# Position network of an attention layer: VectorE's and ScalarE's instructions in a written order, additions two pairs ahead, weighted sums a pair later, first-layer scalings one at a time

## The chip, the cores and the metric

The kernel runs on one core of a Trainium2 chip. A core has five engines that run beside each other and wait for one another by semaphores: TensorE (PE in the profile, its weight loads PEld), VectorE (DVE), ScalarE (ACT), GpSimd (POOL) and SyncE (SP, which issues transfers). The time is that of one execution on the device in microseconds; the median of several runs is compared. Before the change it is 3746.29 us (three runs, 3746.23 to 3746.82).

## The reference

Four layers run one behind the other; the change lies in the first, a deformable attention on x of 2 images, 512 channels, 32 by 32. In it, each of 16 heads (2 images by 8 groups) has 1024 queries and 64 keys. To every score a bias is added which a small network computes from the position of query and key:

```python
pos = grid_q[:, :, None, :] - grid_kv[:, None, :, :]
bias = jnp.sign(pos) * jnp.log1p(jnp.abs(pos))
bias = jax.nn.relu(bias @ cpb_w1 + cpb_b1)      # 2 -> 128
bias = jax.nn.relu(bias @ cpb_w2 + cpb_b2)      # 128 -> 128
bias = (bias @ cpb_w3 + cpb_b3)                 # 128 -> 1
sim = jnp.einsum('bhid,bhjd->bhij', qh, kh) + bias
attn = jax.nn.softmax(sim, axis=-1)
```

That is 16 x 64 x 1024 positions through a hidden layer of 128 by 128, all in float32. The output projection, an MLP and the other three layers (a deformable convolution, a linear attention and an ordinary attention) follow and are not touched.

## The kernel before

The part that matters is `biased_scores` (L828), called the position network here. It works on NP = 8 pairs of heads ("head pairs", index p), and in each on 32 rows j in steps of two. A step (p, j) holds four pairs of keys (t = 0 to 3): the heads 2p and 2p+1, and the keys j, j+1 and j+32, j+33. Counted through, that is 128 steps and 512 pairs; pair n = 64p + 2j + t.

For one key, `hidden` (L862) makes the first layer's output, a tile of 128 hidden units by 1024 queries. The position is separable in x and y, so the first layer is a sum of an x part and a y part: an addition on VectorE (L869), with both parts broadcast, then a relu, on VectorE for the keys 3, 8 and 13 of each sixteen (L876), else on ScalarE (L878). Six such tiles `h` exist, so three pairs.

For a pair, `second_layer` (L881) does the 128 by 128 product on TensorE (L889) in two halves of the output units, `ph`, each of two PSUM banks; three such tiles rotate. A matmul has a tile of 32 columns of the array, and four of them run side by side, two for each key. ScalarE reads the first half with bias and relu into `lo` (L899, two tiles) and the second into `hi` (L901, six tiles, scaled by the size of the last layer's weight). VectorE adds them, `hi = lo * low_w + hi` (L902), which halves the last layer's depth. `last_layer` (L904) then multiplies the four `hi` of a step into `sim` on TensorE (L910). It is called for a step only behind the second pair of the next step.

The x and y parts come from `first_layer` (L511): for a group (p, q) of sixteen rows j it loads four tiles `ab` of 128 by 1024 from DRAM (L521, on SP's queue), and then multiplies each by a weight and adds a bias, in place, on ScalarE (L534). Two groups fit into the pool `cpb_ab`. The next group is called for at j % 16 == 8.

At j = 0 the `sim` of the head pair before is stored (L932, VectorE), at j = 16 the scores themselves are added in (L922, TensorE). In the last four head pairs the softmax of the first four is done beside the network, one step of it after every fourth step (`next(beside)`). `Softmax.parts` (L994): eight transposes on TensorE into a `ph` tile and the maximum (L1012) and the subtraction (L1014) on VectorE; the exponential on ScalarE (L1016); the sum, reciprocal and product on VectorE (L1018 to L1021); at last eight transposes back and a copy on ScalarE (`turn`, L1033).

The order of instructions is set in two ways. A scheduler orders the instructions of an engine by its own view of when their inputs are ready, unless a block `manual_schedule` names that engine: then they stand as the program writes them. Before the change this block names TensorE alone, for the whole of this part. Each engine runs its queue in order, so an instruction that waits holds up all behind it.

Of the kernel before, what the change touches and what calls it, by code (L numbers as in the profile page):

```python
# [11 lines left out]
F32 = mybir.dt.float32  # L12
AF = mybir.ActivationFunctionType
# [497 lines left out]
def first_layer(net, pool, feat, p, q):  # L511

    nc, parts = net.nc, {}
    for i in (2 * p, 2 * p + 1):
        parts[i, q] = []
        for a in range(2):
            t = pool.tile([128, 32, 32], F32, name="ab", tag=f"ab{a}")
            row = feat[16 * a + i : 16 * a + i + 1, :]  # L520
            nc.sync.dma_start(  # L521
                out=t.rearrange("p (u j) i -> p u (j i)", u=2),
                in_=bass.AP(
                    tensor=row.tensor,
                    offset=row.offset + 512 * q,
                    ap=[[0, 128], [HW, 2], [1, 512]],
                ),
            )
            parts[i, q].append(t)
    yield parts  # L530
    for i in (2 * p, 2 * p + 1):
        for a, t in enumerate(parts[i, q]):
            bias = net.vec("cpb_b1") if a == 0 else 0.0
            nc.scalar.activation(t, t, AF.Identity, bias=bias, scale=net.vec("cpb_w1", a))  # L534
    yield parts


class DepthwiseConv:
# [80 lines left out]
def queries_keys_values(net, bn, simT, q_flat, q_pad, kbd, val, feat, first):  # L619
# [5 lines left out]
    with ExitStack() as ctx:  # L625
# [59 lines left out]
        with ExitStack() as part:  # L685
# [109 lines left out]
                            skip_group_check=True,  # L795
                        )
            with net.tc.issue_after(last.ins):
                done = next(weigh)
            for h in range(2):
                r = 64 * h  # L800
                (nc.vector.tensor_copy, nc.scalar.copy)[h](
# [5 lines left out]
            for w, out, factor in ((kw, kbd, 64**-0.5), (vw, val, 1.0)):  # L807
                for q in range(2):
# [14 lines left out]
                        ALU.mult,  # L823
                    )
    return done


def biased_scores(net, q_pad, kbd, feat, w2, simT, first, parts, load_weights):  # L828
# [12 lines left out]
    with ExitStack() as ctx:  # L841
# [20 lines left out]
        nc.vector.tensor_copy(w3[0:64, 30:31], sign[0:64, :])  # L862
        nc.vector.tensor_copy(w3[64:128, 31:32], sign[64:128, :])

        def hidden(i, j, on_vector):
            at_x, at_y = parts[i, j % 32 // 16]
            k = 16 * (j // 32) + j % 16
            h1 = hid1.tile([128, HW], F32, name="h1", tag="h1")
            nc.vector.tensor_tensor(  # L869
                h1.rearrange("p (y x) -> p y x", x=32),  # L870
                at_x[:, k : k + 1, :].to_broadcast([128, 32, 32]),
                at_y[:, k, :].unsqueeze(2).to_broadcast([128, 32, 32]),
                ALU.add,
            )
            if on_vector:
                nc.vector.tensor_scalar(h1, h1, 0.0, None, ALU.max)  # L876
            else:
                nc.scalar.activation(h1, h1, AF.Relu)  # L878
            return h1

        def second_layer(pair):  # L881

            phs = []
            for k in range(2):
                ph = ps_h.tile([128, HW], F32, name="ph", tag="ph")
                for n in range(2):
                    for t in range(4):
                        c0 = 64 * k + 32 * (t % 2)
                        nc.tensor.matmul(  # L889
                            ph[32 * t : 32 * t + 32, half(n)],  # L890
                            lhsT=w2[:, c0 : c0 + 32],
                            rhs=pair[t // 2][:, half(n)],
                            start=True,
                            stop=True,
                            skip_group_check=True,
                        )
                phs.append(ph)
            lo = lows.tile([128, HW], F32, name="lo", tag="lo")
            nc.scalar.activation(lo, phs[0], AF.Relu, bias=b2_lo)  # L899
            hi = highs.tile([128, HW], F32, name="hi", tag="hi")  # L900
            nc.scalar.activation(hi, phs[1], AF.Relu, bias=size_b, scale=size)  # L901
            nc.vector.scalar_tensor_tensor(hi, lo, low_w, hi, ALU.mult, ALU.add)  # L902
            return hi

        def last_layer(sim, j, sums):


            for n in range(2):
                for t in range(4):
                    nc.tensor.matmul(  # L910
                        sim[32 * t : 32 * t + 32, half(n)],
                        lhsT=w3[:, 30 - j : 62 - j],
                        rhs=sums[t][:, half(n)],
                        start=(j == 0),
                        stop=(j == 30),
                        skip_group_check=True,
                    )
# [13 lines left out]
        def store(p, sim):  # L931
            nc.vector.tensor_scalar(simT[:, p, :], sim, net.vec("cpb_b3"), None, ALU.add)  # L932
# [11 lines left out]
        soft = Softmax(net, simT, one, two_banks)  # L944
        beside = chain(*(soft.steps(p) for p in range(CC)))

        pending = None
        sim = None
        hidden_done = 0
        for p, j in [(p, j) for p in range(NP) for j in range(0, 32, 2)]:  # L950
            if j % 16 == 8:
                nxt = 2 * p + j // 16 + 1
                if nxt < 2 * NP:
                    parts.update(list(first_layer(net, first, feat, *divmod(nxt, 2)))[-1])
            sums = []
            for t in range(4):
                pair = []
                for k in range(2):
                    key = j + 32 * (t % 2) + k
                    pair.append(hidden(2 * p + t // 2, key, hidden_done % 16 in (3, 8, 13)))  # L960
                    hidden_done += 1
                sums.append(second_layer(pair))
                if t == 1 and pending is not None:
                    last_layer(sim, *pending[1:])
            if j == 0:
                if pending is not None:
                    store(pending[0], sim)
                sim = ps_sim.tile([128, HW], F32, name="sim", tag="sim")
            elif j == 16:
                scores(p, sim)  # L970
                if p == NP - 1:
                    weights = load_weights()
            pending = (p, j, sums)
            if p >= CC and j % 8 == 4:
                next(beside, None)
        for _ in beside:
            pass
        last_layer(sim, *pending[1:])
# [4 lines left out]
class Softmax:  # L983
# [18 lines left out]
    def parts(self, p):  # L1002
        nc, one = self.net.nc, self.one
        pt = self.banks("pt").rearrange("p (h j) -> p h j", j=64)
        for c in range(8):
            nc.tensor.transpose(
                pt[:, 2 * c : 2 * c + 2, :].rearrange("p h j -> p (h j)"),
                self.simT[:, p, 128 * c : 128 * c + 128],
                self.net.cst("ident"),
            )  # L1010
        m = one("m", 16)
        nc.vector.tensor_reduce(m, pt, AX.X, ALU.max)  # L1012
        e = one("e", HW).rearrange("p (h j) -> p h j", j=64)
        nc.vector.tensor_tensor(e, pt, m.unsqueeze(2).to_broadcast([128, 16, 64]), ALU.subtract)  # L1014
        yield e
        nc.scalar.activation(e, e, AF.Exp)  # L1016
        s = one("s", 16)
        nc.vector.tensor_reduce(s, e, AX.X, ALU.add)  # L1018
        yield e
        nc.vector.reciprocal(s, s)  # L1020
        nc.vector.tensor_tensor(e, e, s.unsqueeze(2).to_broadcast([128, 16, 64]), ALU.mult)  # L1021
        yield e
# [1182 lines left out]
```

## Time and profile before

| | |
|---|---|
| median of the runs | 3746.29 us |
| the profiled execution's own time | 3739.29 us |
| its span, first to last instruction | 3737.4 us |
| mean granted TensorE clock | 0.991 |
| TensorE busy | 3634.7 us (97%) |
| VectorE busy | 2763.5 us (74%) |
| ScalarE busy | 2605.5 us (70%) |
| first and last start of the second layer (L889) | 86.8 and 2116.7 us |
| scalings of `ab` (L534) | 64, of 1.13 to 1.29 us, from 74.3 us on |

The profile lists groups of equal instructions: line, engine, operation, output and inputs, shape, count, busy time and mean duration, then the idle time of the engine just before them and what ended most of it. A timeline row gives start, duration, engine, line, operation, count, and in brackets the idle time before it with its releaser. In the slices of the span (forty, each 93.4 us) TensorE is at nine tenths or more from the second slice to the 32nd, VectorE and ScalarE from the second to the 22nd, which is the position network. A row of windows has start and end, length, then busy time and count of PE, PEld, DVE, ACT and POOL, the granted clock, the share of the DMA engines and GB/s. Matmuls are pipelined and their ends are modelled: a busy share of TensorE is not its rate.

### The profile page before, as it was taken

What the parts mean: (1) busy time and instruction counts of PE and PEld (TensorE: products, weight loads), DVE (VectorE), ACT (ScalarE), POOL (GpSimd) and SP (SyncE); (2) the same over time, 40 slices, a digit from 0 to 9 for tenths busy, and PEclk for the clock granted to TensorE, in tenths of its full rate; (3) what the DMA queues carried; (4) which work ended last, traced back from release to release, by engine and by line L of the source; (5) the groups of instructions that cost most, each with busy time, mean ns of one, the idle gap of its engine ahead of it and who ended that gap; (6) DMA issues with size and microseconds to landing.
All of it is one profiled execution on the core that took longest, in us unless ns stands there. A gap on an engine that the chain in (4) does not pass through costs nothing. (4 is left out here: it accounts for less than half of the span.)

```text
span 3737.4 us, 59880 instructions
## 1 busy us (share of the span) xinstructions
PE 3634.7 (97%) x24332; PEld 1381.4 (37%) x24332; DVE 2763.5 (74%) x3178; ACT 2605.5 (70%) x2877; POOL 436.0 (12%) x692
## 2 busy tenths in 40 slices
PE   7999999999999999999999999999997999989999
PEld 4432322232223232322323344444443455534434
DVE  6999999999999999999999611321257457277776
ACT  7999999999999999999999621021113223257875
POOL 0000000000000000000000000000126024036655
PEclk9999999999999999999999999999998999999999
DMA  3000000000000000000001100012345547036665
GB/s 114 1 24 24 24 1 23 24 24 1 24 24 13 12 24 24 1 24 24 24 1 58 51 12 0 9 33 85 101 137 197 175 144 252 34 102 176 172 180 173
DMA packets 95718, 237.87 MB, mean 64 GB/s; under 512 B 21220, under 2 KB 26852, under 8 KB 92244
## 3 DMA queue, kind: packets, MB, share of 16 engines
q0 software_dynamic: 38160, 112.73, 9.8%
q1 hardware_dynamic: 56132, 117.36, 9.5%
q8 instruction: 193, 3.16, 0.4%
q10 hardware_dynamic: 1152, 3.96, 0.3%
q14 instruction: 81, 0.66, 0.1%
HBM read 157.16 MB, written 9.70 MB: 45 GB/s over the span
## 5 line engine op out<-in xcount | busy, mean ns | idle before, releaser
L889 PE MATMUL ph<-h,w_t 128*32 128x512 f32 x16384 | 1808.1, 593 | 15.7 <-ACT lo L899 6.5
L869 DVE TENSOR_TENSOR h<-ab 128x1024 f32<-128x1024 f32 x1024 | 1205.3, 1217 | 67.5 <-PE ph L889 66.5
L889 PEld LDWEIGHTS ph<-h,w_t 128*32 128x32 f32 x16384 | 547.5, 110 | 1240.0 <-issue 1014.6
L878 ACT ACTIVATE h<-h 128x1024 f32<-128x1024 f32 x832 | 872.2, 1067 | 46.1 <-DVE h L869 42.7
L902 DVE SCALAR_TENSOR_TENSOR hi<-lo,low_w,hi 128x1024 f32<-128x1024 f32 x512 | 654.1, 1278 | 31.7 <-ACT hi L901 30.3
L901 ACT ACTIVATE hi<-ph,size_b,size 128x1024 f32<-128x1024 f32 x512 | 621.3, 1214 | 16.7 <-PE ph L889 12.5
L899 ACT ACTIVATE lo<-ph,vec_t 128x1024 f32<-128x1024 f32 x512 | 571.9, 1117 | 5.9 <-PE ph L889 5.5
L1568 PE MATMUL po<-fold,turned 128*128 128x512 f32 x576 | 270.0, 613 | 3.1 <-DVE dfacc L1576 2.9
L1136 ACT ACTIVATE h<-ph,vec_t 128x512 f32<-128x512 f32 x64 | 44.0, 687 | 312.1 <-PE ph L1128 311.6
L910 PE MATMUL sim<-hi,w 128*32 128x512 f32 x2048 | 251.0, 592 | 0.0
L1197 POOL MEMSET pad<- 128x2312 f32 x2 | 4.1, 2032 | 2075.3 <-PE ph L889 2075.3
L1491 POOL DMA_INDIRECT got<-table,idx x144 | 169.7, 1178 | 555.7 <-DVE sum L1515 273.7
L1128 PE MATMUL ph<-xn,room 128*128 128x512 f32 x512 | 231.0, 594 | 0.0
L1117 PE MATMUL acc<-h,mlp_w_t 128*128 128x512 f32 x512 | 229.8, 592 | 0.0
L1515 DVE SCALAR_TENSOR_TENSOR sum<-got,wts,sum 128x256 f32<-128x256 f32 x432 | 184.6, 479 | 44.8 <-ACT sum L1511 42.1
L2115 DVE TENSOR_REDUCE m<-pl 128x1 f32<-128x1024 f32 x128 | 150.6, 1218 | 84.5 <-PE pl L2003 84.4
L2049 POOL DMA_DIRECT2D aT<-e x344 | 169.0, 499 | 207.0 <-DVE s L2132 97.2
L2121 ACT ACTIVATE e<-pl,m 128x1024 f32<-128x1024 f32 x86 | 95.7, 1114 | 82.8 <-DVE m L2115 56.6
L1568 PEld LDWEIGHTS po<-fold,turned 128*128 128x128 f32 x576 | 108.0, 198 | 114.9 <-issue 109.9
L1542 ACT COPY turned<-pt 128x512 f32<-128x512 f32 x72 | 42.0, 583 | 150.7 <-PE pt L1536 150.7
L1117 PEld LDWEIGHTS acc<-h,mlp_w_t 128*128 128x128 f32 x512 | 97.3, 190 | 122.5 <-issue 122.0
L1128 PEld LDWEIGHTS ph<-xn,room 128*128 128x128 f32 x512 | 96.6, 191 | 117.8 <-issue 117.2
(265 smaller groups left out, 2885.7 us busy)
## 6 DMA issues: line engine op xcount, KB each, us to landing
ab<-feat_d SPq DMA_DIRECT2D x64, 512.0 KB, 4.2
aT<-e SPq DMA_DIRECT2D x344, 64.0 KB, 2.6
aT<-e POOLq DMA_DIRECT2D x344, 64.0 KB, 2.5
room<-in_dc_w_dram SPq DMA_DIRECT2D x9, 1024.0 KB, 4.8
aT<-x_all SPq DMA_DIRECT2D x96, 64.0 KB, 2.7
aT<-x_all POOLq DMA_DIRECT2D x96, 64.0 KB, 2.4
dc_w_t<-in_dc_w_dram SPq DMA_DIRECT2D x5, 1024.0 KB, 4.9
room<-in_mlp_w_dram SPq DMA_DIRECT2D x1, 4096.0 KB, 15.5
```

The source lines that it names most:

```text
L869: nc.vector.tensor_tensor(h1.rearrange("p (y x) -> p y x", x=32), at_x[:, k : k + 1, :].to_broadcast([128, 32, 32]), at_y[:, k, :].unsquee ...
L878: nc.scalar.activation(h1, h1, AF.Relu)
L889: nc.tensor.matmul(ph[32 * t : 32 * t + 32, half(n)], lhsT=w2[:, c0 : c0 + 32], rhs=pair[t // 2][:, half(n)], start=True, stop=True, skip_ ...
L899: nc.scalar.activation(lo, phs[0], AF.Relu, bias=b2_lo)
L901: nc.scalar.activation(hi, phs[1], AF.Relu, bias=size_b, scale=size)
L902: nc.vector.scalar_tensor_tensor(hi, lo, low_w, hi, ALU.mult, ALU.add)
L910: nc.tensor.matmul(sim[32 * t : 32 * t + 32, half(n)], lhsT=w3[:, 30 - j : 62 - j], rhs=sums[t][:, half(n)], start=(j == 0), stop=(j == 30 ...
L1117: nc.tensor.matmul(accs[oc], lhsT=self.w2[:, m, 128 * oc : 128 * oc + 128], rhs=hs[m], start=(m == 0), stop=(m == 15),)
L1128: nc.tensor.matmul(ph, lhsT=self.w1[:, k, 128 * m : 128 * m + 128], rhs=xn[:, k, :], start=(k == 0), stop=(k == CC - 1),)
L1491: nc.gpsimd.indirect_dma_start(out=g.rearrange("p s i -> p (s i)"), out_offset=None, in_=f.table.rearrange("(r t) s i -> r t (s i)", t=2), ...
L1515: nc.vector.scalar_tensor_tensor(t[:, q, :], g[:, s, :], w, t[:, q, :], ALU.mult, ALU.add)
L1568: nc.tensor.matmul(self.out, lhsT=turned[:, at : at + 128], rhs=self.folded.w[k][:, i, :], start=(k == 0 and i == 0), stop=(k == 8 and i = ...
```

## The change

The loop of `biased_scores` now stands in a `manual_schedule` block for VectorE and ScalarE, so their order is that of the program. In the order:

- The two additions of a pair and its relus on VectorE (`added`) come two pairs ahead of the second layer that uses them. The relus on ScalarE stand one behind `lo` and one behind `hi` of the pair two before (`rectified`).
- The weighted sum of a pair comes behind the additions in the next pair (`behind`), no longer with its own.
- The next group's `ab` tiles are called for at j % 16 == 2, and scaled one at a time at the start of the steps j % 16 = 6, 8, 10 and 12 (`next_parts`, and the `yield` that moves into the loop of `first_layer`). The second group's scalings, which before stood ahead of the network, now run inside it.
- In the softmax, the sum of the exponentials moves from the step of the exponential to the next one.

The choice of keys whose relu is on VectorE, the buffers, and the order on TensorE, GpSimd and SyncE stay; each engine has the same instructions as before.

```diff
 def first_layer(...):
         for a, t in enumerate(parts[i, q]):
             bias = net.vec("cpb_b1") if a == 0 else 0.0
             nc.scalar.activation(t, t, AF.Identity, bias=bias, scale=net.vec("cpb_w1", a))
-    yield parts
+            yield parts
...
             with net.tc.issue_after(last.ins):
-                done = next(weigh)
+                done = list(weigh)[-1]
...
+        def added(n):
+            i, first_key = pairs[n]
+            made = []
+            for j in (first_key, first_key + 1):
...
+                nc.vector.tensor_tensor(
+                    h1.rearrange("p (y x) -> p y x", x=32),
...
+                made.append(h1)
+            for u, h1 in enumerate(made):
+                if (2 * n + u) % 16 in ON_VECTOR:
+                    nc.vector.tensor_scalar(h1, h1, 0.0, None, ALU.max)
+            return made
+
+        def rectified(n, u):
+            if n in hiddens and (2 * n + u) % 16 not in ON_VECTOR:
+                h1 = hiddens[n][u]
+                nc.scalar.activation(h1, h1, AF.Relu)
...
+        def weighted(lo, hi):
             nc.vector.scalar_tensor_tensor(hi, lo, low_w, hi, ALU.mult, ALU.add)
...
+        def next_parts(nxt):
+            making = first_layer(net, first, feat, *divmod(nxt, 2))
+            parts.update(next(making))
+            yield
+            yield from making
+
+        pending, sim, hiddens, behind, making = None, None, {}, None, iter(())
+        ahead = 2
+        with net.tc.manual_schedule(
+            engines={mybir.EngineType.DVE, mybir.EngineType.Activation}
+        ):
+            for n in range(ahead):
+                hiddens[n] = added(n)
+                for u in range(2):
+                    rectified(n, u)
+            for p, j in [(p, j) for p in range(NP) for j in range(0, 32, 2)]:
+                if j % 16 == 2:
+                    nxt = 2 * p + j // 16 + 1
+                    if nxt < 2 * NP:
+                        making = next_parts(nxt)
+                if j % 16 > 4 or j % 16 == 2:
+                    next(making, None)
+                sums = []
+                for t in range(4):
+                    n = 64 * p + 2 * j + t
+                    phs = second_layer(hiddens.pop(n))
+                    if n + ahead < len(pairs):
+                        hiddens[n + ahead] = added(n + ahead)
+                    lo = lows.tile([128, HW], F32, name="lo", tag="lo")
+                    nc.scalar.activation(lo, phs[0], AF.Relu, bias=b2_lo)
+                    rectified(n + ahead, 0)
+                    hi = highs.tile([128, HW], F32, name="hi", tag="hi")
+                    nc.scalar.activation(hi, phs[1], AF.Relu, bias=size_b, scale=size)
+                    rectified(n + ahead, 1)
+                    if behind is not None:
+                        weighted(*behind)
+                    behind = lo, hi
+                    sums.append(hi)
+                    if t == 1 and pending is not None:
+                        last_layer(sim, *pending[1:])
...
+            weighted(*behind)
...
         nc.scalar.activation(e, e, AF.Exp)
+        yield e
         s = one("s", 16)
         nc.vector.tensor_reduce(s, e, AX.X, ALU.add)
-        yield e
         nc.vector.reciprocal(s, s)
```

More of the change, by code (lines that the diff above doesn't have):

```diff
@@ L825, in queries_keys_values @@
     return done
+ON_VECTOR = 3, 8, 13
 def biased_scores(net, q_pad, kbd, feat, w2, simT, first, parts, load_weights):
@@ L863, in biased_scores @@
         nc.vector.tensor_copy(w3[64:128, 31:32], sign[64:128, :])
[L865 to L877, printed above, removed]
+        pairs = [
+            (2 * p + t // 2, j + 32 * (t % 2))
+            for p in range(NP)
+            for j in range(0, 32, 2)
+            for t in range(4)
+        ]
+        def added(n):
+            i, first_key = pairs[n]
+            made = []
+            for j in (first_key, first_key + 1):
+                at_x, at_y = parts[i, j % 32 // 16]
+                k = 16 * (j // 32) + j % 16
+                h1 = hid1.tile([128, HW], F32, name="h1", tag="h1")
+                nc.vector.tensor_tensor(
+                    h1.rearrange("p (y x) -> p y x", x=32),
+                    at_x[:, k : k + 1, :].to_broadcast([128, 32, 32]),
+                    at_y[:, k, :].unsqueeze(2).to_broadcast([128, 32, 32]),
+                    ALU.add,
+                )
+                made.append(h1)
[6 more added lines that the diff above has]
+                h1 = hiddens[n][u]
                 nc.scalar.activation(h1, h1, AF.Relu)
-            return h1
         def second_layer(pair):
@@ L897, in second_layer @@
                 phs.append(ph)
[L898 to L901, printed above, removed]
+            return phs
+        def weighted(lo, hi):
             nc.vector.scalar_tensor_tensor(hi, lo, low_w, hi, ALU.mult, ALU.add)
-            return hi
         def last_layer(sim, j, sums):
@@ L945, in biased_scores @@
         beside = chain(*(soft.steps(p) for p in range(CC)))
[L947 to L975, printed above, removed]
@@ new lines, in next_parts @@
+        def next_parts(nxt):
[37 more added lines that the diff above has]
+                        last_layer(sim, *pending[1:])
+                if j == 0:
+                    if pending is not None:
+                        store(pending[0], sim)
+                    sim = ps_sim.tile([128, HW], F32, name="sim", tag="sim")
+                elif j == 16:
+                    scores(p, sim)
+                    if p == NP - 1:
+                        weights = load_weights()
+                pending = (p, j, sums)
+                if p >= CC and j % 8 == 4:
+                    next(beside, None)
+            weighted(*behind)
```

## The prediction

> **What bounds the kernel now.** I read the page first (busy times, slices, groups), then the windows, then TensorE's and ScalarE's timelines inside the position network, where the whole change lies.
>
> ```profile
> span 3737.4 us, 59880 instructions
> PE 3634.7 (97%) x24332; PEld 1381.4 (37%) x24332; DVE 2763.5 (74%) x3178; ACT 2605.5 (70%) x2877; POOL 436.0 (12%) x692
> L889 PE MATMUL ph<-h,w_t 128*32 128x512 f32 x16384 | 1808.1, 593 | 15.7 <-ACT lo L899 6.5
> L869 DVE TENSOR_TENSOR h<-ab 128x1024 f32<-128x1024 f32 x1024 | 1205.3, 1217 | 67.5 <-PE ph L889 66.5
> L878 ACT ACTIVATE h<-h 128x1024 f32<-128x1024 f32 x832 | 872.2, 1067 | 46.1 <-DVE h L869 42.7
> L902 DVE SCALAR_TENSOR_TENSOR hi<-lo,low_w,hi 128x1024 f32<-128x1024 f32 x512 | 654.1, 1278 | 31.7 <-ACT hi L901 30.3
> L901 ACT ACTIVATE hi<-ph,size_b,size 128x1024 f32<-128x1024 f32 x512 | 621.3, 1214 | 16.7 <-PE ph L889 12.5
> L899 ACT ACTIVATE lo<-ph,vec_t 128x1024 f32<-128x1024 f32 x512 | 571.9, 1117 | 5.9 <-PE ph L889 5.5
> ```
>
> The network runs from 84 to 2121 us. The window over it:
>
> ```profile
> 84.00:2121.00 2037.00, 2021.40 (x18562) 627.04 (x18563) 1936.54 (x1764) 1965.79 (x1922) 2.02 (x1) 1.00 0.06 19
> ```
>
> PE is busy 2021.4 us of 2037, DVE 1936.5 and ACT 1965.8: three engines within 5%, so the order in which they serve each other matters. TensorE's timeline tells which one sets the pace:
>
> ```profile
> 330.35 1.90 PE L910 MATMUL sim<-hi,w 128*32 128x512 f32 x16
> 332.07 10.69 PE L889 MATMUL ph<-h,w_t 128*32 128x512 f32 x96
> 343.05 3.64 PE L889 MATMUL ph<-h,w_t 128*32 128x512 f32 x32 [0.30 <-ACT hi L901]
> 346.51 1.90 PE L910 MATMUL sim<-hi,w 128*32 128x512 f32 x16
> 348.23 5.33 PE L889 MATMUL ph<-h,w_t 128*32 128x512 f32 x48
> 354.02 8.96 PE L889 MATMUL ph<-h,w_t 128*32 128x512 f32 x80 [0.46 <-ACT lo L899]
> 362.80 1.90 PE L910 MATMUL sim<-hi,w 128*32 128x512 f32 x16
> ```
>
> One L910 row opens each step of four key pairs. Undisturbed steps are 15.45 us apart (378.25, 393.70, 409.15 follow), most of the 127: 36 groups of four matmuls at 0.429 us, TensorE's own rate. A pair is thus 3.43 us, the last layer 1.72. The two steps shown are 16.16 and 16.29: 0.71 and 0.84 lost. Added over the timeline, beyond 15.45 and beyond the scores (2.02 a head pair) and softmax transposes (1.16 a set), the losses are 25.8 us: 11.7 in the first four head pairs and 14.0 in the last four. Of the 25.8, 20.1 lie at the 14 places where four scalings of `ab` run (some 1.4 each), 5.6 behind the softmax steps. That 25.8 is all that any order can win here. ScalarE at such a place:
>
> ```profile
> 338.70 1.07 ACT L878 ACTIVATE h<-h 128x1024 f32<-128x1024 f32 x1
> 339.64 1.13 ACT L899 ACTIVATE lo<-ph,vec_t 128x1024 f32<-128x1024 f32 x1
> 340.64 1.27 ACT L534 ACTIVATE ab<-ab,vec_t 128x1024 f32<-128x1024 f32 x1
> 341.77 1.23 ACT L901 ACTIVATE hi<-ph,size_b,size 128x1024 f32<-128x1024 f32 x1
> 342.86 1.15 ACT L899 ACTIVATE lo<-ph,vec_t 128x1024 f32<-128x1024 f32 x1
> ```
>
> Starts give the time that each holds the engine: relu 0.95, `lo` 1.00, `hi` 1.09, scaling 1.04 to 1.13 (I take 1.09). The `hi` that ends at 343.00 releases TensorE at 343.05, so ScalarE to TensorE takes 0.05. The other way is read where ScalarE waits:
>
> ```profile
> 2112.18 1.11 ACT L899 ACTIVATE lo<-ph,vec_t 128x1024 f32<-128x1024 f32 x1 [1.54 <-PE ph L889]
> 2113.90 1.21 ACT L901 ACTIVATE hi<-ph,size_b,size 128x1024 f32<-128x1024 f32 x1 [0.60 <-PE ph L889]
> ```
>
> That pair's matmuls start at 2110.21 (call it S): `lo` can start at S+1.97, `hi` at S+3.69. An addition waiting for the freed `h` starts 0.24 behind (2105.28 against 2105.04).
>
> **The change, part by part.** No instruction is added or removed, and the order on TensorE, POOL and SP stays; only DVE and ACT are reordered, in the network alone. So the `ab` loads keep their place in SP's queue; they land 4.2 us after issue, and each scaling is two steps (31 us) or more behind: no price.
>
> *Steady order.* ScalarE now runs, for pair n: `lo`(n), relu(n+2,0), `hi`(n), relu(n+2,1): 1.00+0.95+1.09+0.95 = 3.99 us against TensorE's 3.43. VectorE takes 3 of 16 relus, so in the pairs 2, 4 and 7 of each eight ScalarE has 3.04. TensorE's last layer (1.72) follows pairs 1 and 5. Let the lag be how late `lo`(n) starts behind S+1.97. A full pair adds 0.56, a short one takes 0.39, a last layer takes 1.72. From zero at pair 2: 0.33 at pair 3 (its `hi` before waited for TensorE), 0.88 at 4, 0.49 at 5, 0 at 6, 0.56 at 7, 0.16 at 0, 0.72 at 1, then zero. Two limits: `lo`(n) must be read before the second half of pair n+1 takes its PSUM buffer (three rotate), lag+1.97+1.11+0.05 < 5.15, so lag < 2.02; and relu(n+2,1), done at S+6.12+lag, must precede pair n+2 at S+6.87, so lag < 0.75 where no last layer lies between. The second is tight once in eight pairs, at pair 3: 0.33 against 0.75. DVE needs two additions 2.27, weighted sum 1.20 and at times a relu 0.61: 3.47 or 4.08 a pair against 3.43, its lag stays under 1.4 and clears at each last layer; a sum a pair later is still 2.3 us ahead of its last layer. Steady state costs nothing, as before; cover 0.42 us at pair 3, 64 times.
>
> *Scalings one to a step.* They stand ahead of pair 4, 0, 4, 0. Lags: 0.88+1.09 = 1.97 at pair 4, just inside 2.02; then 1.58, 0.42 (pair 6), 0.98, and with the second scaling 1.68, 2.24 (a last layer follows, so free), 1.06, 0.67 (limit 0.75), and with the third 0.67+0.56+1.09 = 2.32: 0.30 too late. The fourth stays inside. So 0.30 a group where some 1.4 stood; 15 groups (the second group's, until now ahead of the network, comes into it): 4.5 us. Ends: 0, and 1.55 (0.71+0.84 above). I take 0.30, reached with this trace's own durations.
>
> *Softmax steps,* one after every fourth step of the last four head pairs. First: maximum and subtraction (2.4 us) stand in DVE's queue and wait for the transposes; two additions, a relu and the sum of pair 3 are behind, and it comes some 0.1 us before the last layer needs it: 0.05 each. Second: the exponential lands on a lag of 1.28 left by the fourth scaling: 1.28+0.95-2.02 = 0.21, three times, and 1.6 the first time, with the table load. Third: sum, reciprocal and product (2.69 us by their starts) push the sum of pair 3 to 11.2 us behind that pair's start, the last layer wants it at 10.3: 0.9, four times. Fourth: the copy fits in the transposes' own 1.16. Storing a head pair (1.28 on DVE) leaves 0.6 of cover. Together 0.2+2.2+3.6 = 6.0, ends 0 and 12.
>
> The table load is a row of 1.28 us at 1149.34, and the exponential starts at 1150.63, right behind. [...]
>
> *Start and end.* ScalarE loses four scalings ahead of the first pair, but that pair waits for DVE's first addition at 84.40, behind the copies of `val`: 0, ends plus and minus 1. The end is the same chain of `hi`, sum, last layer.
>
> Sum: 4.5+6.0 = 10.5 us of losses for 25.8: 15.3 less. The profiled execution took 3739.3 us (span 3737.4 and 1.9 around it), so 3724.0; the median shown is 7.0 above it: 3731.0.
>
> **The rivals.** *Nothing of the 25.8 stays* (chance 0.12): the lags run 0.3 lower, every wait is covered: 3720.5. For it: 0.30 is a small overshoot. Against: the 0.9 behind the third softmax step.
>
> *Scalings cost the same one by one as together* (0.16): ScalarE owes 4.4 us a group whatever the spacing, and the four steps have 15.6 us of its work in 15.45; 15 times 1.43 and 6.0 are 27.5, 1.7 over: 3748. Against: the pairs' own lag returns to zero in between, up to 0.88 only.
>
> *Slower: ScalarE's fixed order misses pair 5* (0.14). At pair 3 relu(5,1) stands behind `hi`(3), which waits for TensorE; a scheduler may move it, a fixed order may not. Cover 0.42; each 0.1 us beyond costs 64 times 0.1 = 6.4. From 0.66 us on it eats the gain; at 0.8 it is 64x0.38 = 24.3: 3755. For it: ACT waits for `h` 42.7 us now, so hand-overs are close. Against: the durations agree within 0.05.
>
> *ScalarE is the bound, not TensorE* (0.02). Then its idle of 46.1+16.7+5.9 = 68.7 us is the gain: 3677.6. Against: steps stand at exactly 15.45 while ScalarE idles in them. [...]
>
> **How the numbers follow.** The forecast has 0.56, its own range 3723 to 3740. The range 3719 to 3750 takes in the first two rivals and leaves out most of the slower one. A measurement tells about 0.2%, 7.5 us. Faster: 0.56 less its edge of 0.03, plus 0.12 and 0.02, 0.67; same: 0.16 and most of the edge, 0.18; slower 0.15.
>
> **What would show it.** In TensorE's timeline: steps of 15.45 with no pair of 16.2 and 16.3 at the scalings; a single `ab` row between a relu and `lo`; a wait of L910 for the weighted sum at the third softmax step; one larger wait at the first exponential. The prediction is wrong if steps without scalings exceed 15.45, or if each scaling still costs 0.3 or more.

## The result, and the profile after

The changed kernel takes 3726.53 us (median of six runs, 3723.5 to 3728.36), the kernel before 3746.26 us in as many runs beside it (3744.27 to 3748.74). The ratio is 0.9946, with a 95% interval of 0.9933 to 0.9959: 19.7 us less, 15 to 25 by the interval. That is inside the range and on the side that was forecast; the forecast itself, 3731.0, was 4.5 us too high. In a later session, nine runs of the kernel before (median 3741.07) and five of the changed one (3724.24) lie 16.8 us apart.

The page of the changed kernel, by lines that answer to those shown of before (L908 was L889, L883 was L869, L898 was L878, L920 was L902, L997 was L901, L994 was L899):

```profile
span 3725.5 us, 59739 instructions
PE 3630.9 (97%) x24332; PEld 1394.9 (37%) x24332; DVE 2772.1 (74%) x3178; ACT 2587.1 (69%) x2877; POOL 441.7 (12%) x692
L908 PE MATMUL ph<-h,w_t 128*32 128x512 f32 x16384 | 1797.1, 593 | 7.3 <-ACT h L898 3.9
L883 DVE TENSOR_TENSOR h<-ab 128x1024 f32<-128x1024 f32 x1024 | 1205.9, 1219 | 45.4 <-PE ph L908 43.4
L898 ACT ACTIVATE h<-h 128x1024 f32<-128x1024 f32 x832 | 925.6, 1113 | 7.0 <-DVE size L857 6.2
L920 DVE SCALAR_TENSOR_TENSOR hi<-lo,low_w,hi 128x1024 f32<-128x1024 f32 x512 | 654.8, 1279 | 20.5 <-ACT hi L997 20.0
L997 ACT ACTIVATE hi<-ph,size_b,size 128x1024 f32<-128x1024 f32 x512 | 644.7, 1259 | 21.6 <-PE ph L908 21.6
L994 ACT ACTIVATE lo<-ph,vec_t 128x1024 f32<-128x1024 f32 x512 | 596.2, 1164 | 43.5 <-PE ph L908 38.7
```

Counts are the same. What moved is the idle time: the second layer's fell from 15.7 to 7.3 us. ScalarE's relus hardly wait for VectorE's additions any more (42.7 us before, 0.7 now; the 6.2 shown are at the start, for `size`); ScalarE now waits for TensorE instead, 38.7 us at `lo` and 21.6 at `hi`. The mean durations of ScalarE's three operations rose by 46, 45 and 47 ns, which is taken up in the last section.

The window over the network in the changed kernel (the columns are explained above, with the profile before):

```profile
84.00:2104.00 2020.00, 2012.48 (x18554) 639.57 (x18554) 1945.60 (x1764) 1950.34 (x1925) 2.02 (x1) 1.00 0.06 19
```

TensorE is not busy in 7.5 us of 2020, where it was 15.6 of 2037; the clock is 1.00 in both.

TensorE's timeline of the changed kernel at a third scaling, the step that opens at 407.45:

```profile
407.45 1.90 PE L927 MATMUL sim<-hi,w 128*32 128x512 f32 x16
...
421.52 1.92 PE L908 MATMUL ph<-h,w_t 128*32 128x512 f32 x16 [0.16 <-ACT lo L994]
423.26 1.90 PE L927 MATMUL sim<-hi,w 128*32 128x512 f32 x16
...
438.71 1.90 PE L927 MATMUL sim<-hi,w 128*32 128x512 f32 x16
```

One step is 15.81 us, 0.36 over, and the next is 15.45 again, as 80 of the 126 steps are. Before, such a place had two steps of 16.16 and 16.29.

Where the time went is counted over the 126 steps between the first regular L927 row (110.22) and the last (2092.28). At 15.45 each, with eight times 2.01 for the scores and eight times 1.16 for transposes, they need 1972.06 us. The 0.5 us that the kernel before loses in its first two steps are counted in here; the prediction's 25.8 left them out.

| | before | after |
|---|---|---|
| first to last step, us | 1998.39 | 1982.06 |
| losses beyond 1972.06, us | 26.3 | 10.0 |
| from the last step's row to the end of the span, us | 1628.9 | 1633.3 |
| profiled execution's own time, us | 3739.29 | 3727.43 |

The network gained 16.3 us, where 15.3 were forecast. The stage behind it, which the change doesn't touch, took 4.4 us longer in this execution, so that the profiled times differ by 11.9 only. Its length lay between 1625.8 and 1634.0 in the traced executions of these kernels, whatever their order in the network. One execution's total thus carries a scatter of up to 8 us that has nothing to do with the change. The network's losses are steadier: 10.0 and 9.6 us in the two traced executions of the changed kernel.

### The profile page after: what moved, and what is told of

Read it like the earlier page. It is cut to its first block, busy times and chain, and to the rows that moved or that the text cites. A ratio compares the mean times of both kernels' runs of the same rounds, so it can differ in the third digit from the quotient of the medians.

```text
span 3725.5 us, 59739 instructions
## 1 busy us (share of the span) xinstructions
PE 3630.9 (97%) x24332; PEld 1394.9 (37%) x24332; DVE 2772.1 (74%) x3178; ACT 2587.1 (69%) x2877; POOL 441.7 (12%) x692
## 5 line engine op out<-in xcount | busy, mean ns | idle before, releaser
L908 PE MATMUL ph<-h,w_t 128*32 128x512 f32 x16384 | 1797.1, 593 | 7.3 <-ACT h L898 3.9
L883 DVE TENSOR_TENSOR h<-ab 128x1024 f32<-128x1024 f32 x1024 | 1205.9, 1219 | 45.4 <-PE ph L908 43.4
L908 PEld LDWEIGHTS ph<-h,w_t 128*32 128x32 f32 x16384 | 560.0, 110 | 1209.5 <-issue 1071.8
L898 ACT ACTIVATE h<-h 128x1024 f32<-128x1024 f32 x832 | 925.6, 1113 | 7.0 <-DVE size L857 6.2
L920 DVE SCALAR_TENSOR_TENSOR hi<-lo,low_w,hi 128x1024 f32<-128x1024 f32 x512 | 654.8, 1279 | 20.5 <-ACT hi L997 20.0
L997 ACT ACTIVATE hi<-ph,size_b,size 128x1024 f32<-128x1024 f32 x512 | 644.7, 1259 | 21.6 <-PE ph L908 21.6
L994 ACT ACTIVATE lo<-ph,vec_t 128x1024 f32<-128x1024 f32 x512 | 596.2, 1164 | 43.5 <-PE ph L908 38.7
L927 PE MATMUL sim<-hi,w 128*32 128x512 f32 x2048 | 249.5, 592 | 0.0
```

Source lines behind the costliest of these rows:

```text
L883: nc.vector.tensor_tensor(h1.rearrange("p (y x) -> p y x", x=32), at_x[:, k : k + 1, :].to_broadcast([128, 32, 32]), at_y[:, k, :].unsquee ...
L908: nc.tensor.matmul(ph[32 * t : 32 * t + 32, half(n)], lhsT=w2[:, c0 : c0 + 32], rhs=pair[t // 2][:, half(n)], start=True, stop=True, skip_ ...
L927: nc.tensor.matmul(sim[32 * t : 32 * t + 32, half(n)], lhsT=w3[:, 30 - j : 62 - j], rhs=sums[t][:, half(n)], start=(j == 0), stop=(j == 30 ...
```

## The experiments

Losses below are counted in the same way, from one trace of each kernel. The first six kernels below were run once each, so that where their totals are close, the losses speak and not the total; those with a ratio were run several times.

### Four scalings in one place

```diff
-                if j % 16 > 4 or j % 16 == 2:
+                if j % 16 == 2:
                     next(making, None)
+                elif j % 16 == 6:
+                    some(making, 5)
```

Against the changed kernel: the written order stays, but the four scalings of a group stand together again.

> The changed kernel with one part undone: the four scalings of a group stand together ahead of the first pair of the step j % 16 = 6, in the same written order. Theory A (what TensorE loses is set by how late ScalarE comes to a PSUM half, limit 2.02 us, and a scaling is 1.09 of that): the lag at that pair is 0.88 + 4 x 1.09 = 5.24, so 3.2 us are lost in each of 15 groups, 48 in place of 5.4; the network loses about 52 us and the time is near 3769. Rival B (the written order as such brings the gain, the place of the scalings is incidental): network losses stay near 9.5 us, time 3727.

Measured: 3775.32 us (before on that chip 3737.94), losses 59.8 us. TensorE's timeline at two such places:

```profile
405.79 2.80 PE L908 MATMUL ph<-h,w_t 128*32 128x512 f32 x16 [3.05 <-ACT lo L996]
408.35 2.79 PE L927 MATMUL sim<-hi,w 128*32 128x512 f32 x16
...
924.00 1.93 PE L908 MATMUL ph<-h,w_t 128*32 128x512 f32 x16 [3.04 <-ACT lo L996]
925.75 1.47 PE L927 MATMUL sim<-hi,w 128*32 128x512 f32 x12
```

Seven of fifteen groups lose 3.25 us (3.2 was expected); in four of these the softmax transposes stand in the same step, and their 1.16 us lies within the 3.25. The other eight lose 4.7 to 5.7: there the sixteen matmuls behind the wait take longer, in the first place shown 2.56 us (405.79 to 408.35) where the second has 1.75. Behind the first wait shown the granted clock was 0.66 over 5 us, behind the second 1.00 (last section). What follows: the place of the scalings in ScalarE's queue is worth tens of microseconds in a fixed order, and the kernel before, at some 1.4 a group, had its four already spread a little by the scheduler.

### The spread calls alone, under the scheduler

```diff
-    yield parts
+            yield parts
...
-            if j % 16 == 8:
+            if j % 16 == 2:
                 nxt = 2 * p + j // 16 + 1
                 if nxt < 2 * NP:
-                    parts.update(list(first_layer(net, first, feat, *divmod(nxt, 2)))[-1])
+                    making = next_parts(nxt)
+            if j % 16 > 4 or j % 16 == 2:
+                next(making, None)
```

Against the kernel before: no order is written, but the program calls for the scalings one to a step.

> The kernel before, orders left to the scheduler, with one part of the change alone: the program calls for the scalings one to a step, at j % 16 = 6, 8, 10 and 12. As built, the scheduler still puts them within a few pairs, as before. Theory A: the place on ScalarE decides, so the network loses what it lost before, 24 to 27 us, time 3744 to 3748. Rival C (calling them early and one by one is enough): losses near 10 us, time near 3730.

Measured: 3736.87 us beside 3737.94, losses 26.3 us as before. ScalarE's and TensorE's timelines of this kernel:

```profile
462.24 1.17 ACT L534 ACTIVATE ab<-ab,vec_t 128x1024 f32<-128x1024 f32 x1
...
477.43 1.21 ACT L534 ACTIVATE ab<-ab,vec_t 128x1024 f32<-128x1024 f32 x1
```

```profile
468.73 3.64 PE L889 MATMUL ph<-h,w_t 128*32 128x512 f32 x32 [0.29 <-ACT hi L901]
...
479.70 1.93 PE L889 MATMUL ph<-h,w_t 128*32 128x512 f32 x16 [0.46 <-ACT lo L899]
```

The three scalings in this stretch (the second at 466.31) start 0.5 us later than in the kernel before (461.71, 465.78, 476.91), as its whole network does (first L910 row at 110.59 instead of 110.11), and the two waits are the ones seen there. The calls moved, the instructions did not. The spreading worked only through a written order.

### One engine's order at a time

```diff
-            engines={mybir.EngineType.DVE, mybir.EngineType.Activation}
+            engines={mybir.EngineType.Activation}
```

> The changed program with only ScalarE's order written; VectorE's is left to the scheduler. Theory A: ScalarE holds the scalings, so nearly all of the gain is here: network losses 9 to 13 us, time 3726 to 3731. Rival B (both written orders are needed, the additions two pairs ahead above all): losses 18 to 26 us, time 3736 to 3746.

Measured: 3724.82 us beside 3737.94, losses 10.0 us, as with both. TensorE's timeline of this kernel at the third scaling that was shown for the changed kernel:

```profile
409.23 1.90 PE L927 MATMUL sim<-hi,w 128*32 128x512 f32 x16
...
425.04 1.90 PE L927 MATMUL sim<-hi,w 128*32 128x512 f32 x16
```

The step is 15.81 us here too. Eleven third scalings cost 0.36, the first exponential 1.60 and the others 0.18; the first softmax steps lose 0.6 each, and the third ones nothing.

```diff
-            engines={mybir.EngineType.DVE, mybir.EngineType.Activation}
+            engines={mybir.EngineType.DVE}
```

> The changed program with only VectorE's order written; ScalarE's is left to the scheduler, which as built puts the scalings within a few pairs. Theory A: network losses stay at 20 to 27 us, time 3741 to 3748. Rival B (VectorE's order brings the gain): losses near 10 us, time near 3728.

Measured: 3744.92 us beside 3737.94 (one run each), losses 24.4 us. The waits are back where the kernel before had them; the first of the two here:

```profile
470.67 3.64 PE L908 MATMUL ph<-h,w_t 128*32 128x512 f32 x32 [0.30 <-ACT hi L997]
```

So ScalarE's order carries the gain, and VectorE's alone is worth 1.9 us in the network (26.3 less 24.4), which a single total doesn't show.

### The other two parts: sum in its own pair, one pair ahead

```diff
-                    if behind is not None:
-                        weighted(*behind)
-                    behind = lo, hi
+                    weighted(lo, hi)
```

> The changed kernel with one part undone: the weighted sum of a pair stands on VectorE in its own pair, behind the additions for two pairs later, and no longer a pair later. Theory A (in a written order a wait holds up all that stands behind it): the sum waits for hi of its pair, the next additions stand behind the sum, ScalarE's next relu waits for them and its next hi stands behind that relu: a ring of 0.05 + 1.20 + 1.22 + 0.07 + 0.95 + 1.21 = 4.7 us a pair, but in one of eight (its relu is on VectorE) some 3.0; 35.9 us for eight pairs in place of 30.9, so 64 x 5 = 320 us longer (250 to 400), time near 4045. Rival D (the last layer needs the sum 2 us later, so its place costs nothing): time near 3727.

Measured: 4086.63 us; the network takes 364.7 us longer than in the changed kernel (+320 expected, 250 to 400). ScalarE's and VectorE's timelines of this kernel:

```profile
600.78 1.19 ACT L997 ACTIVATE hi<-ph,size_b,size 128x1024 f32<-128x1024 f32 x1
...
604.46 1.06 ACT L898 ACTIVATE h<-h 128x1024 f32<-128x1024 f32 x1 [0.54 <-DVE h L883]
605.43 1.19 ACT L997 ACTIVATE hi<-ph,size_b,size 128x1024 f32<-128x1024 f32 x1
```

```profile
602.01 1.28 DVE L920 SCALAR_TENSOR_TENSOR hi<-lo,low_w,hi 128x1024 f32<-128x1024 f32 x1 [1.08 <-ACT hi L997]
603.21 2.35 DVE L883 TENSOR_TENSOR h<-ab 128x1024 f32<-128x1024 f32 x2
```

Read as a ring: the sum waits for `hi` (end 601.97, start 602.01), the additions stand behind it on VectorE, the relu waits for the first of them (604.46), and the next `hi` stands behind that relu. One round is 4.65 us (600.78 to 605.43), where 4.7 was expected and TensorE needs 3.43.

```diff
-        ahead = 2
+        ahead = 1
```

> The changed kernel with additions and relus one pair ahead in place of two. Theory A: relu(n+1,1) stands behind hi(n), which waits for pair n on TensorE, and is done at S + 6.12, so the next pair starts there and not at S + 3.43; with the shorter pairs (relu on VectorE) eight pairs take 4.08 + 3 x 6.12 + 5.89 + 5.15 + 2 x 6.12 = 45.7 us in place of 30.9, so 64 x 14.8 = 950 us longer (800 to 1050), time near 4670. Rival E (two additions and a relu take 3.3 us, a pair 3.43, so one pair ahead is enough): time 3727 to 3760.

Measured: 4674.59 us, the network 937.5 us longer (+950 expected). A wait for `h` in TensorE's timeline:

```profile
623.71 6.46 PE L908 MATMUL ph<-h,w_t 128*32 128x512 f32 x32 [2.24 <-ACT h L898]
```

Eight pairs take 45.69 us where the matmuls behind the wait run at their usual rate (716.55 to 762.24), and 45.7 was reckoned. That the total comes out so near is partly luck: behind 29 of the 48 waits of 2.24 us the matmuls were slower (the row shown is 6.46 us long, at a granted clock of 0.66; last section), such a round took 47.15 us, and together they add some 41 us, while the scores and transposes, 25 us, fall into waits.

What follows from the two: a fixed order without the additions two pairs ahead is 25% slower than the changed kernel, and one without the later sum 10%. By themselves these two bring little beyond what the scheduler had: VectorE's written order, which holds both, gained 1.9 us. They are the price of entry for writing the order.

### The scaling ahead of the second pair

```diff
-                if j % 16 > 4 or j % 16 == 2:
+                if j % 16 == 2:
                     next(making, None)
                 sums = []
                 for t in range(4):
                     n = 64 * p + 2 * j + t
+                    if t == 1 and j % 16 > 4:
+                        next(making, None)
```

Against the changed kernel: a scaling stands before the pair whose last layer gives ScalarE 1.72 us to recover.

> The changed kernel with each scaling moved by one pair, from the head of its step to ahead of the step's second pair, behind which the last layer gives ScalarE 1.72 us. Theory A: the lag there is 0.49 or 0.72 + 1.09 = 1.58 or 1.81, its limit with the last layer behind it 3.7, and it is back under 0.75 two pairs later: no loss at the scalings. Network losses 9.5 - 5.4 = 4 us (3 to 5), time 5.4 below the changed kernel's, near 3721. Rival B: as the changed kernel, 3726.5.

Measured: 3720.46 us (3717.59 to 3721.92), ratio to before 0.9937 (0.992 to 0.9953). The losses are 9.2 us, not 4. TensorE's timeline around the second head pair's scores (row 480.52):

```profile
471.23 0.60 PE L927 MATMUL sim<-hi,w 128*32 128x512 f32 x2
471.41 0.60 PE L908 MATMUL ph<-h,w_t 128*32 128x512 f32 x2
471.66 1.63 PE L927 MATMUL sim<-hi,w 128*32 128x512 f32 x12
472.95 0.60 PE L908 MATMUL ph<-h,w_t 128*32 128x512 f32 x2
473.13 0.60 PE L927 MATMUL sim<-hi,w 128*32 128x512 f32 x2
...
480.52 1.94 PE L939 MATMUL sim<-room,kbd 128*64 128x512 f32 x8
...
489.29 1.04 PE L927 MATMUL sim<-hi,w 128*32 128x512 f32 x8
```

No step is over 15.45 at the third scaling any more, yet the scores cost 2.60 (471.23 to 489.29, 18.06 less 15.45) instead of 2.01, and the transposes 1.52 to 1.59 instead of 1.16. The rows show what is different. Two of the sixteen matmuls of the last layer start at 471.23, and two of the second layer, which stand ahead of them in the program, only at 471.41; at 472.95 the next second layer starts before the last two of the last layer (473.13). I read this as two of the four column tiles of 32 running behind the other two; no row names the tile. From its first start to its last end the last layer takes 2.50 us (471.23 to 473.73), where a row in step takes 1.90: 0.60 more, and the scores cost 0.59 more. The step ahead of the row doesn't show it (15.45 us, 455.78 to 471.23); by my reading it is paid at the operations that span several tiles, the scores (64 wide) and the transposes (128 wide). The exponentials got dearer too, 1.97 and three times 0.56 where the changed kernel has 1.61 and 0.18; the fourth scaling stands in the same step, closer to them, which may be the reason. Four times 0.59 at the scores, 1.6 at the transposes, 3.6 at the exponentials, 0.40 in the last head pair and 0.5 each at the first group and at the third softmax steps are 9.0 of the 9.2. The expectation had counted only what comes past a limit at once.

### Each remaining loss attacked

```diff
+            loaded = small.tile([128, 1], F32, name="loaded", tag="loaded")
+            nc.scalar.activation(loaded, w3_hi, AF.Exp)
...
-                if p >= CC and j % 8 == 4:
+                if p >= CC and (j % 8 == 4 or j == 14):
                     next(beside, None)
...
         nc.vector.reciprocal(s, s)
+        yield e
         nc.vector.tensor_tensor(e, e, s.unsqueeze(2).to_broadcast([128, 16, 64]), ALU.mult)
```

On top of the kernel above: a tiny exponential ahead of the network loads ScalarE's table, and the third softmax step is cut in two.

> As the run before it, and two more: a tiny exponential ahead of the network so that its table is loaded while ScalarE waits for the first addition, and the softmax's sum and reciprocal at j = 14, the product alone at j = 20. Theory A: no table load within the network (1.4 less), the exponential lands on a lag of 0.88 (0.2 less, four times), no late weighted sum (0.4 less, four times): network losses below 1.5 us, time near 3718. Rival B: as the changed kernel, 3726.5.

Measured: 3722.28 us (3719.2 to 3724.58), ratio 0.9941 (0.9925 to 0.9958); losses 6.2 us, not under 1.5. The table's stall is gone, as TensorE's timeline of this kernel shows at the first exponential:

```profile
1191.44 1.99 PE L927 MATMUL sim<-hi,w 128*32 128x512 f32 x16
...
1207.46 1.90 PE L927 MATMUL sim<-hi,w 128*32 128x512 f32 x16
```

The step that ends at 1207.46 loses 0.57, as much as the three exponentials without a load in the kernel shown before this one (0.56): so it was the load that made the first one dearer. Four exponentials are 2.3 us, the scores, still at 2.60, another 2.4, transposes of 1.34 to 1.51 another 0.9, and the first four head pairs lose 0.7 more around the scalings. The cut of the third softmax step took its 0.17 away.

### The scalings on VectorE, and the changed kernel beside it

```diff
-def first_layer(net, pool, feat, p, q):
+def first_layer(net, pool, feat, p, q, on_vector=False):
...
+            elif a == 0:
+                nc.vector.tensor_scalar(t, t, scale, bias, ALU.mult, ALU.add)
+            else:
+                nc.vector.tensor_scalar(t, t, scale, None, ALU.mult)
             yield parts
...
-                    if t == 1 and j % 16 > 4:
-                        next(making, None)
                     phs = second_layer(hiddens.pop(n))
+                    if t == 3 and j % 16 > 4:
+                        next(making, None)
```

On top of the last one: the scalings inside the network run on VectorE, ahead of the additions of a step's last pair.

> As the eighth kernel (table loaded ahead, softmax sum at j = 14 and product at j = 20), but the scalings inside the network run on VectorE, one to a step, ahead of the additions of the step's last pair, where VectorE waits 0.2 to 0.3 us for TensorE now. Theory A: ScalarE's lag stays under 0.88 and no relu is late; VectorE takes some 0.6 us a scaling (its relu of the same size holds it 0.6), two in eight pairs, in place of 1.3 us of slack there. Network losses below 3 us (after the change 10.0, in the eighth 6.2), time 7 to 9 below the changed kernel's on this chip. Rival F (VectorE, busy 96%, becomes late in its place: weighted sums or relus): losses 10 or more, time no better than the changed kernel's.

> The changed kernel again, on the same chip as the run before it, for their comparison: ratio to the kernel before 0.9933 to 0.9959 as measured, network losses 10.0 us.

Measured on the same chip: 3720.45 us with the scalings on VectorE (3717.32 to 3723.39, five runs; ratio to before 0.9945, 0.9931 to 0.9958), 3724.24 for the changed kernel (3723.05 to 3727.91, five runs; 0.9955, 0.9941 to 0.9969). The 3.8 us between the medians are 0.1% and the runs overlap by 0.3 us, so the totals alone don't settle it; the losses in the network, 4.7 against 9.6 us, say a like amount. Losses and time both fall short of what was expected (below 3, and 7 to 9 us less). The step that lost 0.36 in the changed kernel is now 15.45 long (406.09 to 421.54).

One scaling is 0.74 or, with its bias, 0.81 us on VectorE, against a median of 1.24 on ScalarE in the changed kernel. No scaling costs anything in the first four head pairs. What is left are 0.71 at the first scores (the row ahead of them, at 217.97, is 0.71 longer than 1.90) and, in each of the last four head pairs, 0.79 at the step of the exponential and 0.21 at the scores. ScalarE's timeline at the first 0.79:

```profile
1195.18 1.06 ACT L904 ACTIVATE h<-h 128x1024 f32<-128x1024 f32 x1 [0.52 <-DVE h L889]
...
1198.18 1.05 ACT L1067 ACTIVATE e<-e 128x1024 f32<-128x1024 f32 x1
```

The fourth scaling now delays an addition, a relu waits 0.52 us for it, and the exponential stands three instructions on. That this meeting makes the 0.79 was not tried by moving one of the two. The 0.21 comes behind the step into which the sum of the softmax was moved: the last layer's row ahead of the scores is 2.10 us long there (1217.47) instead of 1.90, 0.20 more. Whether the moved sum makes it longer wasn't tried.

## Why the prediction was right, point by point

- **The bound** held. TensorE's steps of 15.45 us are the floor in the kernel before and in every kernel here that keeps the additions two pairs ahead and the sum a pair later. The rival that made ScalarE the bound fell: with 60.3 us of ScalarE's idle time now in waits for TensorE (38.7 and 21.6), it is TensorE that sets the pace.
- **Steady order, no cost:** right. Steps without a scaling or a softmax step are 15.45, so pair 5 is in time, and the slower rival with it falls. That the two limits are real, and of about the size given, is shown by the orders which break them: four scalings in one place pass the first (3.25 us a group, 3.2 from the limit), additions one pair ahead the second (45.69 us for eight pairs, 45.7 reckoned).
- **Scalings, 0.30 at the third of each group, 4.5 us:** right in mechanism and nearly in size. It is the third that costs most: 0.36 for eight groups, 0.28 for the first group of each of the last four head pairs, about 0.36 for the three others, 5.1 in all. The first, put "just inside" its limit, is 0.05 outside it in ten groups (376.50 to 392.00 is 15.50 us), another 0.5. The size was off by the durations, as ScalarE's timeline of the changed kernel shows:

```profile
169.09 1.33 ACT L534 ACTIVATE ab<-ab,vec_t 128x1024 f32<-128x1024 f32 x1
170.23 1.21 ACT L994 ACTIVATE lo<-ph,vec_t 128x1024 f32<-128x1024 f32 x1
```

  The starts are as priced, but this `lo` takes 1.21 where 1.11 was taken; TensorE starts at 171.48, right behind its end at 171.44. "Cost the same one by one as together" falls with that (1.4 a group).
- **The exponential, 1.6 with the table and 0.2 for the others:** measured 1.61 and three times 0.18. ScalarE's timeline:

```profile
1200.52 1.21 ACT L898 ACTIVATE h<-h 128x1024 f32<-128x1024 f32 x1
1201.75 1.28 ACT L1057 ACT_TABLE_LOAD   x1
1203.04 1.06 ACT L1057 ACTIVATE e<-e 128x1024 f32<-128x1024 f32 x1
1204.01 1.10 ACT L994 ACTIVATE lo<-ph,vec_t 128x1024 f32<-128x1024 f32 x1
```

  The load takes 1.28 us; it starts 0.02 behind the relu's end and the exponential 0.01 behind the load.
- **First softmax step, 0.05 each:** measured none (1143.21 follows its step by 15.45 and 1.16).
- **Third softmax step, 0.9 four times, 3.6 us:** this is the term that failed; it is 1.4. Two things were wrong in it. VectorE's lag at pair 3 was put too high, so the sum was placed 11.2 us behind that pair's start. VectorE's timeline of the changed kernel around it:

```profile
1260.62 2.36 DVE L883 TENSOR_TENSOR h<-ab 128x1024 f32<-128x1024 f32 x2 [0.16 <-PE ph L908]
...
1269.77 1.28 DVE L920 SCALAR_TENSOR_TENSOR hi<-lo,low_w,hi 128x1024 f32<-128x1024 f32 x1
```

  The additions start at 1260.62, 0.21 behind the pair's start at 1260.41, because the freed buffer is that of the pair before; the sum ends at 1271.05, 10.64 behind. And the loss is not taken where it arises, as TensorE's timeline shows:

```profile
1255.26 1.90 PE L927 MATMUL sim<-hi,w 128*32 128x512 f32 x16
...
1270.76 2.25 PE L927 MATMUL sim<-hi,w 128*32 128x512 f32 x16
...
1286.21 2.25 PE L927 MATMUL sim<-hi,w 128*32 128x512 f32 x16
1287.93 14.61 PE L908 MATMUL ph<-h,w_t 128*32 128x512 f32 x128
1302.36 1.90 PE L927 MATMUL sim<-hi,w 128*32 128x512 f32 x16
```

  The step that ends at 1270.76 is 0.05 over, as the same step is in the first four head pairs, where no softmax runs: that is the first scaling. But the row lengthens from 1.90 to 2.25 us, which I read as the column tile with the late sum of pair 3 running 0.35 behind the others; it is as long a step later, and in the step that ends at 1302.36 0.70 is lost, 0.36 of it the scaling's if that costs what it does elsewhere. In the last head pair, where no scaling follows, 0.40 is lost at the transposes (17.01 from 2075.27 to 2092.28, where 15.45 and 1.16 are due).
- **Start, 0:** the first step opens 0.11 later, and 0.84 is lost by the third L927 row (141.96); before, some 0.5 was lost there. By the same reading column tiles run behind one another from the start: the row at 125.67 ends at 128.41, 0.84 later than one in step would, and the step from it to 141.96 is 16.29 us, 0.84 over. Inside the bounds of plus and minus 1.
- **The sum:** 5.1 and 0.5 at the scalings, 2.15 at the exponentials, 1.4 and 0.84 are 10.0, what was measured. 10.5 was forecast: 2.2 too much at the third softmax steps, 0.2 at the first, 1.1 too little at the scalings and 0.84 at the start. That these nearly balance is luck.
- **The total:** 15.3 of gain forecast, 16.3 found in the network. Half of the difference is the smaller losses (10.0, not 10.5), half the start of the kernel before, which the 25.8 had left out. The 7.0 us that the prediction added from the profiled execution to the median didn't come back: the profiled execution of after lies 0.9 above its median. The two medians differ by 19.7, and by 16.8 in the later session; the 3.4 us beyond the network's 16.3 in the first are within the scatter of single executions, and no trace shows where they lie.
- **"Nothing of the 25.8 stays":** fell, with 10.0 left. Even the kernel made to remove each loss kept 4.7.

## What to carry to other kernels

When three engines are nearly full, find TensorE's undisturbed step in its timeline first: what lies above it (26.3 us in the kernel before, above steps of 15.45) is all that an order can win, and it can be listed loss by loss. Then write down, for each pair, by how much each producer is behind (a lag) and where it has slack (a last layer, a pair with less work); an extra instruction whose lag was gone before the next limit cost nothing here (the steps of a second and a fourth scaling, 392.00 to 407.45 and 423.26 to 438.71, are 15.45 us), and four in a row cost eight times as much as four apart (3.25 against 0.41 us a group). The written order also had to decouple its engines, by working ahead and consuming late: with the sum in its own pair a hand-over closed a ring of 4.65 us a round where TensorE needs 3.43; and asking the scheduler for the same spread through the order of calls moved nothing here.

## What the runs showed of the hardware

**ScalarE's durations grew in stretches without a gap.** By the table load shown above a relu's row has gone from 1.05 to 1.20 us, `lo` from 1.10 to 1.25 and `hi` from 1.19 to 1.35, while the starts stay 0.95, 1.00 and 1.09 apart; TensorE was released at the longer end (171.44 and 171.48 above). Behind the load the rows are 1.06 and 1.10 again, behind a relu of 1.21; behind two waits for TensorE, of 0.31 and 0.60 us, they were shorter too (a relu of 1.09 at 128.77 ahead of the waits, 1.05 at 132.99 behind them). In the kernel with the scalings on VectorE ScalarE idles 117 us of its network window (84 to 2098), where the changed kernel has 70, and its mean relu is back to 1064 ns from 1113:

```profile
L904 ACT ACTIVATE h<-h 128x1024 f32<-128x1024 f32 x832 | 885.5, 1064 | 12.1 <-DVE h L889 12.0
```

The time by which successive rows overlap is thus 0.10 to 0.26 us here. The cause was not looked for; up to 0.1 us later at a tight hand-over (the `lo` of 1.21 above, where 1.11 was taken) is most likely, by my estimate, what made 0.30 into 0.36 at the scalings.

**A last layer's row longer than 1.90 us was paid for at the scores or transposes behind it.** The weight loads came four at a time, 128 by 32 each, every 0.43 us (PEld rows of the kernel before at 2104.21, 2104.64 and 2105.07, 0.13 us long). That the four column tiles wait separately, and that an operation over several of them waits for the last, is my reading of the rows; it was not shown tile by tile. What the traces show is the length of the row, from its first start to its last end, and what the next scores or transposes cost beyond 2.01 and 1.16 us:

| kernel, and start of the row | longer than 1.90 by, us | the scores or transposes behind it dearer by, us |
|---|---|---|
| scalings on VectorE, 1217.47 | 0.20 | 0.20 |
| scalings ahead of the second pair, 1128.06 | 0.35 | 0.36 |
| changed kernel, 2075.27 | 0.40 | 0.40 |
| scalings ahead of the second pair, 471.23 | 0.60 | 0.59 |
| scalings on VectorE, 217.97 | 0.71 | 0.71 |

In the kernel with the scalings ahead of the second pair TensorE did not start its matmuls strictly in the program's order, as the text on the kernel before has it for every engine: the rows at 472.95 and 473.13 above stand the other way round in the program.

**TensorE's granted clock was lower, 0.66, behind some waits of 2 or 3 us.** The windows of the kernel with four scalings in one place, the 5 us behind the two waits shown there, and of the kernel one pair ahead behind two waits of 2.24 us (columns: start and end, length, PE, PEld, DVE, ACT and POOL busy, granted clock, DMA share, GB/s):

```profile
406.00:411.00 5.00, 5.00 (x36) 1.29 (x32) 3.19 (x3) 5.00 (x6) 0.00 (x0) 0.66 0.01 3
924.00:929.00 5.00, 5.00 (x48) 1.59 (x52) 2.98 (x3) 5.00 (x6) 0.00 (x0) 1.00 0.01 2
```

```profile
623.71:628.71 5.00, 5.00 (x28) 1.24 (x28) 3.29 (x4) 1.70 (x2) 0.00 (x0) 0.66 0.23 71
716.55:721.55 5.00, 4.56 (x32) 1.05 (x32) 3.29 (x4) 4.12 (x4) 0.00 (x0) 1.00 0.00 0
```

Behind 3.05 us of idle the granted clock was 0.66 over 5 us and 36 matmuls ran, behind 3.04 it stayed at 1.00 and 48 ran; behind 2.24 us it was 0.66 in one place and 1.00 in another. The rows give the other waits. Of the fifteen of the first kernel, eight of the eleven of 3.00 to 3.05 us were followed by sixteen matmuls in 2.36 to 3.62 us; behind the other three, and behind all four of 1.9, these took 1.92 or 1.93. Of 48 waits of 2.24 us in the second, 29 were followed by rows of 28 to 32 matmuls in 5.22 to 6.50 us, where 28 take 3.63 behind the others. Waits of equal length went both ways; what decides was not shown.
